# Layer 1 of a graph attention network: rows of each tile divided among TensorE, VectorE and ScalarE by a small search, diagonals in pairs of rows, an earlier store of x and a moved softmax

## The chip, the cores and the metric

The kernel runs on one core of a Trainium2 chip. The metric is device time in microseconds (us) of one execution, median of several runs. Before the change it is 5647.59 us (11 runs, 5640.64 to 5659.87).

## The reference, cut to what matters

A graph of 10,000 nodes and 170,000 directed edges (80,000 random pairs in both directions and one self-loop per node); x is 10,000 x 768, everything in float32. Two attention layers (the first with 4 heads of 256 channels, the second with one head of 768) and a layer norm at the end:

```python
def gat_conv(x, edge_index, W, a_src, a_dst, bias, heads, out_ch, concat):
    xl = (x @ W).reshape(n, heads, out_ch)
    e = leaky_relu(alpha_src[src] + alpha_dst[dst], 0.2)   # alpha: xl times a, per head
    e = exp(e - segment_max(e, dst)[dst])
    alpha = e / (segment_sum(e, dst)[dst] + 1e-16)
    return segment_sum(xl[src] * alpha[:, :, None], dst) + bias
h  = relu(layer_norm(gat_conv(x, W1, ...))) + (x @ Wr1 + br1)        # layer 1, 1024 wide
h2 = layer_norm(gat_conv(h, W2, ...)) + (h @ Wr2 + br2)              # layer 2, 768 wide
out = layernorm(x + h2)
```

## The kernel before

**Stages.** First, until about 884 us of the profile, x @ W1 and the logits go into a table in HBM, `table1` (one row of 1024 + 9 numbers a node), while the nodes are sorted by degree. Then layer 1 (`ordered_layer1`) runs to about 3460 us, and layer 2 (`ordered_layer2`) to the end at 5649 us. The change is in layer 1 alone.

**Tiles of layer 1.** The sorted nodes make 79 tiles of 128. Each partition holds one node. A tile has `SLOTS[t]` = n slots: slot 0 is the node itself, the others are its neighbours, so that a tile takes n gathers of 128 table rows (529 KB each). Worked out from `slot_counts`, the sizes in the order of work climb from 8 to 26, then comes one tile of 41, and then they fall from 27 to 9. How many tiles have each size: 8, 9, 10: one each; 11 and 12: 3 each; 13: 5; 14: 6; 15: 8; 16: 7; 17: 8; 18: 7; 19: 7; 20: 6; 21: 4; 22: 4; 23 and 24: 2 each; 25, 26, 27, 41: one each; 1377 slots in all. The tile of 41 doesn't fit the ring and goes in three parts through `attend_parts`.

**The ring.** Gathered rows lie in a ring of `RING1` = 29 slots in SBUF. `Ring.fetch` (L449, its DMAs at L424) issues the gather for slot q on GpSimd (POOL) once the row that lay there 29 slots earlier is used. Gathers are issued strictly in order.

**The softmax of a tile.** `weights_of(t)` is a generator. Its first step is `logits` (L471 to L490: add, leaky relu, maximum, subtraction on VectorE, exp at L485 on ScalarE); it needs all n rows of the tile. Its second step is `normalised` (L492 to L499, VectorE) and the diagonals and matmuls of the first two rows that TensorE takes; its third step those of the remaining rows. It is called inside the loop of the tile before, so that program order fixes where it stands in each engine's queue: `logits` before row n-3 of the running tile is weighed, `normalised` before row n-2, the third step at the start of the next tile, behind the instruction group `deviation`.

**Three ways to add a row.** Each row of a tile has to be multiplied by its four weights and added to the accumulator `acc` in PSUM:

- on TensorE (L719 to L732): ScalarE makes four diagonal matrices of 128 x 128 from the weights (L723), TensorE multiplies the row by them and adds in PSUM (L729). The first `on_pe(t)` rows go this way: at most 4. They start the accumulation, so VectorE adds its first row only when they are done.
- on VectorE alone (L519): four instructions that multiply and add.
- shared: ScalarE multiplies the row in place (`multiply`, L508, four instructions), VectorE adds it (L515, one instruction).

Of the rows that TensorE leaves, every fourth, beginning with the first, is done by VectorE alone (`shared(t, k)`, `SHARE` = 4). ScalarE multiplies `LEAD` = 3 rows ahead of VectorE (`multiplied`).

**Around the rows.** Tile t - 1 is finished at the start of tile t: statistics on VectorE (L572, L574) and their square root on ScalarE (L576, L577), then `h` (L586, L588, L800), its transposes on TensorE (L699), copies of these on ScalarE (L700), the product with `w2` (L817, `to_layer2`) and the copy of its result (L759) into `row`, which is stored. The transposes of x for tile t (L699 too, copies L700) and the product with `wr1` (L171) stand in between. Two PSUM buffers named `half` serve the transposes and the product with `w2`. x rows of the next tile are gathered into the single buffer `xt` by the event `next_x`, two rows into the loop, and stored to `x_d` for layer 2 by `from_x` (L707) at the start of the next tile.

**Order.** The scope is a `manual_schedule`: every engine runs its instructions in the order of the program, and waits by semaphores where data of other engines is needed. DMAs on the SP queue are issued in program order: `row` (L761), x (L707), `h1_d` (L812).

## Time and profile before

| | us |
|---|---|
| median of 11 runs | 5647.59 |
| profiled execution, its own time | 5650.69 |
| its span | 5648.8 |
| layer 1, about 884 to 3460 | 2576 |
| of that, busy: TensorE / VectorE / ScalarE / POOL | 2267 / 2221 / 1858 / 1479 |

How long one tile of layer 1 takes, as the distance from one L800 to the next in the timeline (means over the tiles of that size):

| rows n | 13 | 14 | 15 | 16 | 17 | 18 | 19 | 20 | 21 | 22 | 23 | 24 | 25 | 26 | 27 |
|---|---|---|---|---|---|---|---|---|---|---|---|---|---|---|---|
| us | 25.9 | 26.3 | 28.2 | 28.3 | 29.6 | 30.6 | 31.9 | 34.1 | 35.8 | 40.0 | 42.4 | 43.5 | 45.4 | 41.9 | 52.1 |

How to read the profile: times are microseconds; PE is TensorE, PEld its weight loads, DVE VectorE, ACT ScalarE, POOL GpSimd, SP the engine that issues most DMAs. A line of the timeline has the start, the length, the engine, the line of the kernel, the operation, the tiles it writes and reads, shapes, how many instructions were merged, and in brackets how long the engine was idle before and what ended that.

### The profile page before, as it was taken

To read this page: it belongs to the slowest core of one execution; us is meant where nothing else is said; L and a number is where in the kernel's file an instruction comes from. 1 tells how busy PE (TensorE), PEld (TensorE's weight loads), DVE (VectorE), ACT (ScalarE), POOL (GpSimd) and SP (SyncE) were. 2 spreads that over 40 slices of the span, in tenths; PEclk is the share of its full clock that TensorE was granted. 3 is DMA by queue.
4 is the path that set the end of the run, shared out by engine and by line. 5 is a ranking of instruction groups with operands and counts; after the bars stand their busy time and mean duration, and the time that the engine had idled before them with its cause. 6 is when DMAs were issued, how large, how long until landed. Compare 5 with 4: busy or idle time off the path is not lost. (4 is left out here: it accounts for less than half of the span.)

```text
span 5648.8 us, 59565 instructions
## 1 busy us (share of the span) xinstructions
PE 4905.3 (87%) x15188; PEld 2901.7 (51%) x15191; DVE 4289.5 (76%) x7729; ACT 2810.0 (50%) x8184; POOL 3225.7 (57%) x3159
## 2 busy tenths in 40 slices
PE   9999996999999865789999999998887757788898
PEld 3444443555555543455555555655555535455565
DVE  5883344999998886888999995886766656777787
ACT  3443344777777766777877763332222222222232
POOL 3447454555666655566666543666656656666563
PEclk9999998999999987899999999998888878888899
DMA  4333627899999986899999986998888878888885
GB/s 155 121 101 86 93 92 264 320 337 353 359 371 357 352 317 221 320 348 353 364 352 356 334 289 254 324 333 303 308 290 287 290 244 301 301 295 299 302 320 201
DMA packets 474307, 1591.37 MB, mean 282 GB/s; under 512 B 118328, under 2 KB 122488, under 8 KB 473959
## 3 DMA queue, kind: packets, MB, share of 16 engines
q0 software_dynamic: 322384, 1286.62, 63.9%
q1 hardware_dynamic: 149520, 297.43, 15.7%
q10 hardware_dynamic: 2054, 3.42, 0.2%
q8 instruction: 128, 2.10, 0.1%
q14 instruction: 221, 1.80, 0.1%
HBM read 1431.80 MB, written 177.29 MB: 285 GB/s over the span
## 5 line engine op out<-in xcount | busy, mean ns | idle before, releaser
L424 POOL DMA_INDIRECT ring<-table,slots x2675 | 2646.4, 989 | 1757.7 <-issue 520.7
L519 DVE SCALAR_TENSOR_TENSOR acc<-ring,e,acc 128x512 f32<-128x512 f32 (+1 forms) x2530 | 1578.3, 624 | 150.8 <-PE acc L729 49.6
L508 ACT ACTIVATE ring<-ring,e 128x256 f32<-128x256 f32 x3284 | 1337.6, 508 | 0.0
L515 DVE TENSOR_TENSOR acc<-acc,ring 128x1024 f32<-128x1024 f32 x801 | 985.6, 1230 | 71.0 <-issue 0.9
L942 PE MATMUL big<-wr,w 128*128 128x512 f32 (+1 forms) x2464 | 895.1, 508 | 160.9 <-issue 159.1
L928 PE MATMUL big<-ring,diagonals 128*128 128x256 f32 x2754 | 735.9, 426 | 187.3 <-issue 150.0
L171 PE MATMUL big<-w,xT 128*128 128x512 f32 x1896 | 826.2, 598 | 21.9 <-DMA w<-in_W_dram 9.2
L171 PE MATMUL big<-wr,xT 128*128 128x512 f32 x1896 | 834.4, 597 | 0.2 <-issue 0.2
L817 PE MATMUL half<-w,hT 128*128 128x512 f32 (+1 forms) x2528 | 830.5, 486 | 0.0
L942 PEld LDWEIGHTS big<-wr,w 128*128 128x128 f32 x2464 | 487.2, 199 | 536.6 <-issue 505.0
L928 PEld LDWEIGHTS big<-ring,diagonals 128*128 128x128 f32 x2754 | 583.2, 215 | 345.4 <-issue 217.8
L927 ACT ACTIVATE diagonals<-ident,e 128x128 f32<-128x128 f32 x1377 | 424.4, 388 | 639.5 <-remote 252.8
L729 PE MATMUL acc<-ring,diagonals 128*128 128x256 f32 x1912 | 485.6, 412 | 223.4 <-ACT diagonals L723 165.8
L817 PEld LDWEIGHTS half<-w,hT 128*128 128x128 f32 x2528 | 477.8, 189 | 372.7 <-issue 329.1
L171 PEld LDWEIGHTS big<-w,xT 128*128 128x128 f32 x1896 | 362.3, 192 | 481.4 <-issue 464.3
L171 PEld LDWEIGHTS big<-wr,xT 128*128 128x128 f32 x1896 | 357.5, 192 | 420.8 <-issue 420.8
L729 PEld LDWEIGHTS acc<-ring,diagonals 128*128 128x128 f32 x1912 | 391.9, 208 | 309.7 <-ACT diagonals L723 182.8
L576 ACT ACTIVATE sd<-mv,eps 128x1 f32<-128x1 f32 x237 | 69.3, 292 | 715.2 <-DVE mv L574 439.0
L723 ACT ACTIVATE diagonals<-ident,e 128x128 f32<-128x128 f32 x956 | 292.8, 387 | 206.7 <-DVE e L499 143.4
L660 DVE TENSOR_TENSOR scr<-big,ad_b 128x1024 f32<-128x1024 f32 x79 | 96.7, 1224 | 375.6 <-ACT row L657 311.2
L665 POOL TENSOR_TENSOR row<-row,none 128x1024 f32<-128x1024 f32 x79 | 187.2, 2369 | 261.4 <-ACT row L657 255.7
L485 ACT ACTIVATE e<-e 128x68 f32<-128x68 f32 (+29 forms) x160 | 38.2, 239 | 574.1 <-DVE e L484 283.6
(172 smaller groups left out, 3633.1 us busy)
## 6 DMA issues: line engine op xcount, KB each, us to landing
ring<-table,slots POOLq DMA_INDIRECT x2675
table<-row SPq DMA_DIRECT2D x79, 516.0 KB
h_d<-hT SPq DMA_DIRECT2D x79, 512.0 KB
w<-h_d SPq DMA_DIRECT2D x77, 512.0 KB
table<-row SPq DMA_DIRECT2D x79, 385.0 KB
ring<-table SPq DMA_DIRECT2D x79, 385.0 KB
xT<-in_x_cols_dram SPq DMA_DIRECT2D x79, 384.0 KB
x_d<-xt SPq DMA_DIRECT2D x79, 384.0 KB
```

The source lines that it names most:

```text
L171: nc.tensor.matmul(p[:, c:e], aT[:, j, :], w[:, j, c:e], start=(j == 0), stop=(j == k - 1))
L424: nc.gpsimd.indirect_dma_start(out=to, out_offset=None, in_=table, in_offset=bass.IndirectOffsetOnAxis(ap=index, axis=0), **more)
L508: nc.scalar.activation(row[:, s], row[:, s], AF.Copy, scale=e[:, h:h + 1])
L515: nc.vector.tensor_add(acc[:, :c], acc[:, :c], row[:, :c])
L519: nc.vector.scalar_tensor_tensor(acc[:, s], row[:, s], e[:, h:h + 1], (acc if first is None else first)[:, s], op0=OP.mult, op1=OP.add)
L665: nc.gpsimd.tensor_add(row[:, :C1], row[:, :C1], b1_b)
L723: nc.scalar.activation(diagonals[:, k * H1 + i, :], ident, AF.Copy, scale=e[:, k, i:i + 1])
L729: nc.tensor.matmul(acc[:, c:d], diagonals[:, k * H1 + i, :], ring.slot(q + k)[:, c:d], start=(k == 0 and c % BANK == 0), stop=(k == m - 1 ...
L817: nc.tensor.matmul(q, hT[:, j, :], w2[:, j, c:c + q.shape[1]], start=(j == 0), stop=(j == K1 - 1))
L927: nc.scalar.activation(diagonals[:, k % G, :], ident, AF.Copy, scale=e[:, k, :])
L928: nc.tensor.matmul(to, diagonals[:, k % G, :], ring.slot(FIRST[t] + k)[:, ON_PE2:C2], start=False, stop=(k == n - 1), skip_group_check=True)
L942: nc.tensor.matmul(r[:, c:d], hT[:, j, :], wr2[:, j, c:d], start=False, stop=(j == K1 - 1 and (d < C2 or not whole(t))), skip_group_check= ...
```

## The change

- **Shares.** `balanced(n)` searches over all pairs (rows on TensorE, rows on VectorE alone) for the one whose longest engine, by seven constants (microseconds a tile and a row), is shortest. `on_pe` and `shared` take their numbers from it. Rows on VectorE alone are spread over the tile, the first one standing first as before.
- **Diagonals.** `summed` is now a generator that takes two rows at a time, each pair in one of two buffers of eight matrices; before, one buffer held sixteen. Each pair is a step of `weights_of`.
- **Store of x.** `fetch_x` itself issues the store to `x_d`, directly behind the gather that fills `xt`.
- **Softmax.** `logits` of the next tile stands before row `begin` of the running tile, `normalised` with the first pair before row `begin + 2`, further pairs one row later each. `begin` is n - 5, later where the ring makes the next tile's last row late, and at most n - 2. Where `begin` is n - 2, `normalised` falls into the next tile and stands behind its statistics (L572, L574). In tiles where the softmax was done in time, the remaining diagonals and the first shared row of the new tile are put ahead of the square root of the statistics on ScalarE.

Worked out by `balanced`, rows on TensorE / VectorE alone / shared, before and after:

| n | before | after | | n | before | after |
|---|---|---|---|---|---|---|
| 13 | 1 / 3 / 9 | 1 / 1 / 11 | | 20 | 4 / 4 / 12 | 4 / 3 / 13 |
| 14 | 2 / 3 / 9 | 1 / 1 / 12 | | 21 | 4 / 5 / 12 | 4 / 3 / 14 |
| 15 | 2 / 4 / 9 | 1 / 1 / 13 | | 22 | 4 / 5 / 13 | 5 / 3 / 14 |
| 16 | 3 / 4 / 9 | 2 / 1 / 13 | | 23 | 4 / 5 / 14 | 5 / 3 / 15 |
| 17 | 3 / 4 / 10 | 2 / 2 / 13 | | 24 | 4 / 5 / 15 | 6 / 4 / 14 |
| 18 | 4 / 4 / 10 | 3 / 2 / 13 | | 25 | 4 / 6 / 15 | 6 / 4 / 15 |
| 19 | 4 / 4 / 11 | 3 / 2 / 14 | | 26, 27 | 4 / 6 / 16, 17 | 7 / 5 / 14, 15 |

Tiles of 8 to 12 rows go from 1 / 2 or 3 / rest to 1 / 1 / rest. Over the whole layer (without the tile of 41): on TensorE 227 to 202 rows, VectorE alone 308 to 149, shared 801 to 985.

```diff
+EARLY = 5
+PE_FIXED, PE_ROW = 24.0, 1.86
+DVE_FIXED, DVE_ROW, DVE_SUM = 7.9, 2.15, 1.31
+ACT_FIXED, ACT_ROW, ACT_DIAGONAL = 4.0, 1.65, 1.21
...
             def fetch_x(t):
                 xt = pool.tile([P, D0], F32, name="xt")
                 gather(xt, x[:, :], nodes(t))
+                nc.sync.dma_start(x_d[t], xt)
                 return xt
...
             def from_x(t):
                 xT = pool.tile([P, K0, P], F32, name="xT")
-                moves = halves(xT, xt)
-                nc.sync.dma_start(x_d[t], xt)
-                return xT, moves
+                return xT, halves(xT, xt)
...
+            def balanced(n):
+                def longest(pe, alone):
+                    both = n - pe - alone
+                    return max(PE_FIXED + PE_ROW * pe, DVE_FIXED + DVE_SUM * both + DVE_ROW * alone,
+                               ACT_FIXED + ACT_DIAGONAL * pe + ACT_ROW * both)
+                return min(((pe, alone) for pe in range(1, n) for alone in range(1, n - pe + 1)),
+                           key=lambda s: (longest(*s), s))
+            split = {n: balanced(n) for n in set(SLOTS)}
             def on_pe(t):
-                return min(max(SLOTS[t] // 2 - 5, 1), ON_PE1, SLOTS[t])
+                return split[SLOTS[t]][0]
...
+            def summed(acc, e, q, m):
+                for lo in range(0, m, 2):
+                    hi = min(lo + 2, m)
+                    diagonals = pool.tile([P, 2 * H1, P], F32, name="diagonals", bufs=2)
...
+                    yield acc
...
-                diagonals = pool.tile([P, ON_PE1 * H1, P], F32, name="diagonals")
-                for lo, hi in ((0, min(m, 2)), (min(m, 2), m)):
-                    summed(acc, diagonals, e, FIRST[t], lo, hi, m)
-                    yield acc
+                yield from summed(acc, e, FIRST[t], m)
             def shared(t, k):
-                return (k - on_pe(t)) % SHARE > 0
+                m, alone = split[SLOTS[t]]
+                return (k - m) * alone % (SLOTS[t] - m) >= alone
...
-                if whole and not ready:
-                    ahead = weights_of(t)
-                    ready += itertools.islice(ahead, 2)
...
-                if whole:
+                if len(ready) == 2:
                     e, acc = ready
+                    for _ in ahead:
+                        pass
+                    multiplied(first + 2)
                 if last:
                     r_before, means = last
                     stats = deviation(small, pieces(means[:, :C1], BANK))
+                if whole and len(ready) < 2:
+                    if not ready:
+                        ahead = weights_of(t)
+                    ready += itertools.islice(ahead, 2 - len(ready))
+                    e, acc = ready
                 for _ in ahead:
                     pass
...
+                begin = n
                 if whole and t + 1 < NT and SLOTS[t + 1] + LEAD <= ring.size:
+                    begin = min(max(n - EARLY, n + SLOTS[t + 1] - ring.size + EARLY), n - 2)
                     ahead = weights_of(t + 1)
                 for k in range(n if whole else 0):
                     multiplied(k + 1 + LEAD)
-                    if n - LEAD <= k < n - LEAD + 2:
-                        ready += itertools.islice(ahead, 1)
+                    if k == begin or k > begin + 1:
+                        step = list(itertools.islice(ahead, 1))
+                        ready += step[:2 - len(ready)]
                     if k >= first:
                         weigh(acc, ring.slot(FIRST[t] + k), e[:, k], DH1, shared=shared(t, k))
...
-                ready += itertools.islice(ahead, max(2 - len(ready), 0))
```

More of the change, by code (lines that the diff above doesn't have):

```diff
@@ L712, in ordered_layer1 @@
             g1_b, be1_b = (spread(pool, v, n) for v, n in ((g1, "g1"), (be1, "be1")))
-            def on_pe(t):
-                return min(max(SLOTS[t] // 2 - 5, 1), ON_PE1, SLOTS[t])
-            def summed(acc, diagonals, e, q, lo, hi, m):
-                for k in range(lo, hi):
-                    for i in range(H1):
-                        nc.scalar.activation(diagonals[:, k * H1 + i, :], ident, AF.Copy,
-                                             scale=e[:, k, i:i + 1])
-                for k in range(lo, hi):
-                    for i in range(H1):
-                        c, d = i * DH1, (i + 1) * DH1
-                        nc.tensor.matmul(acc[:, c:d], diagonals[:, k * H1 + i, :], ring.slot(q + k)[:, c:d],
-                                         start=(k == 0 and c % BANK == 0),
-                                         stop=(k == m - 1 and (d % BANK == 0 or d == C1)),
-                                         skip_group_check=True)
+            def balanced(n):
[5 more added lines that the diff above has]
+                           key=lambda s: (longest(*s), s))
@@ new lines, in ordered_layer1 @@
+            split = {n: balanced(n) for n in set(SLOTS)}
+            def on_pe(t):
+                return split[SLOTS[t]][0]
[3 more added lines that the diff above has]
+                    diagonals = pool.tile([P, 2 * H1, P], F32, name="diagonals", bufs=2)
+                    for k in range(lo, hi):
+                        for i in range(H1):
+                            nc.scalar.activation(diagonals[:, (k - lo) * H1 + i, :], ident, AF.Copy,
+                                                 scale=e[:, k, i:i + 1])
+                    for k in range(lo, hi):
+                        for i in range(H1):
+                            c, d = i * DH1, (i + 1) * DH1
+                            nc.tensor.matmul(acc[:, c:d], diagonals[:, (k - lo) * H1 + i, :],
+                                             ring.slot(q + k)[:, c:d],
+                                             start=(k == 0 and c % BANK == 0),
+                                             stop=(k == m - 1 and (d % BANK == 0 or d == C1)),
+                                             skip_group_check=True)
+                    yield acc
@@ L842, in some @@
                         m = min(ON_PE1, e.shape[1])
-                        diagonals = pool.tile([P, ON_PE1 * H1, P], F32, name="diagonals")
-                        summed(sums, diagonals, e, q, 0, m, m)
+                        for _ in summed(sums, e, q, m):
+                            pass
                         return sums, m
```

## The prediction

> **What bounds the kernel now.** I read the table of stretches first, then the waits, then the timeline of a tile of 15 rows and of one of 23.
>
> ```profile
> core 0: us, PE busy (x) PEld busy (x) DVE busy (x) ACT busy (x) POOL busy (x), PEclk, DMA share, GB/s
> 1500.00:1800.00 300.00, 283.17 (x962) 172.34 (x961) 271.72 (x443) 235.73 (x640) 191.75 (x188) 0.99 0.98 364
> 2200.00:2500.00 300.00, 223.42 (x714) 137.93 (x714) 244.48 (x381) 214.64 (x571) 171.10 (x173) 0.85 0.89 323
> ```
>
> In the first stretch (tiles of 16 to 20 rows) TensorE, VectorE and the DMA engines are all above 90% and ScalarE at 79%: nothing there has much room. In the second (27 down to 22 rows) every engine is idle for a fifth or more, and TensorE's granted clock is 0.85: here a chain of waits sets the time.
>
> ```profile
> 3116.68 0.25 ACT L485 ACTIVATE e<-e 128x60 f32<-128x60 f32 x1 [3.23 <-DVE e L188]
> 3119.21 2.44 ACT L723 ACTIVATE diagonals<-ident,e 128x128 f32<-128x128 f32 x8 [2.28 <-DVE total L498]
> 3124.03 0.29 ACT L576 ACTIVATE sd<-mv,eps 128x1 f32<-128x1 f32 x1 [2.37 <-DVE mv L574]
> 3124.46 0.84 ACT L759 COPY row<-half 128x512 f32<-128x512 f32 x2
> 3127.67 0.86 ACT L700 COPY xT<-half 128x512 f32<-128x512 f32 x2 [0.76 <-PE half L699]
> ...
> 3100.34 1.75 PE L699 MATMUL half<-ident,h 128*128 128x128 f32 x8 [2.29 <-DVE h L800]
> 3101.88 11.51 PE L171 MATMUL big<-wr,xT 128*128 128x512 f32 x24
> 3128.31 1.09 PE L699 MATMUL half<-ident,h 128*128 128x128 f32 x8 [0.46 <-ACT xT L700]
> ```
>
> A tile of 15 rows. VectorE shows no idle time at all in its timeline from 3098.97 (one L800) to 3126.88 (the next): it is the bound. A row alone takes 2.16 us there (3100.11 to 3102.27), a shared row 1.31 (three in 3.94). ScalarE is idle in three places, each time for a VectorE result: 3.2 us before the exp, 2.3 before the diagonals, 2.4 before the square root. The first is true slack; the other two come from the order of the queue. The TensorE lines show one more thing: after 2.29 us of idleness the same eight transposes take 1.75 instead of 1.09, and L171 about 1 us longer; the clock was granted at half for 3.4 us.
>
> ```profile
> 2384.12 0.21 DVE L477 TENSOR_TENSOR e<-ring 128x48 f32<-128x48 f32 x1 [2.24 <-issue]
> 2388.71 0.25 DVE L499 TENSOR_TENSOR e<-e,total 128x88 f32<-128x88 f32 x1
> 2389.51 9.38 PE L729 MATMUL acc<-ring,diagonals 128*128 128x256 f32 x32 [9.33 <-ACT diagonals L723]
> 2391.41 1.29 DVE L572 BATCH_NORM_STATS2 st<-acc 128x6 f32<-128x512 f32 x2
> 2393.05 1.28 DVE L586 SCALAR_TENSOR_TENSOR h<-acc,mv,g 128x1024 f32<-128x1024 f32 x1
> 2395.84 1.22 DVE L800 SCALAR_TENSOR_TENSOR h<-h,big 128x1024 f32<-128x1024 f32 x1
> 2398.93 1.54 DVE L519 SCALAR_TENSOR_TENSOR acc<-ring,e,acc 128x256 f32<-128x256 f32 x3 [1.88 <-PE acc L729]
> ```
>
> A tile of 23 rows passing to one of 22. The softmax ends at 2388.96 (L499); TensorE, idle for 9.3 us and so at half clock, takes 9.4 us for its four rows; VectorE covers this with its last rows, statistics and h, and still waits 1.88 us before its first row. It also waits for the last gathered row (2.24 us before L477): that gather was issued at 2375.94.
>
> **The change part by part.** The sum is made against the profiled execution, 5650.7 us, which is 3.1 above the median.
>
> *Up to 13 rows (14 tiles).* TensorE keeps one row, VectorE changes two rows from alone to shared: 2 x (2.16 - 1.31) = 1.7 us less for 13 rows. TensorE is next: 24.6 us a tile (966.46 to 991.04 in its timeline, without pauses but one of 0.46), and tiles of 13 take 25.9. The early tiles go at TensorE's pace already. Bounds: 0 to -10 us. I take -3, as ScalarE (below) takes part of it.
>
> *14 to 16 rows (21 tiles).* VectorE: for 15 rows 4 alone + 9 shared become 1 + 13, that is -3 x 2.16 + 4 x 1.31 = -1.2 us; the same for 16, and -0.4 for 14. TensorE loses a row, 1.73 us (3.46 for two). ScalarE gains four shared rows of 1.61 us (24 instructions in 9.69) and loses four diagonals (1.22): +5.2. Of the 8 us that it idles, which remain? From the end of `normalised` (time 0): three shared rows on VectorE (3.93) and statistics (1.58) put the square root at 5.5; before it ScalarE now does diagonals (1.2) and one row (1.6) and waits 2.6 for it. Then root 0.43, copies of `row` 0.73, a wait of some 0.5 for TensorE's transposes of x (the row that stood in between is now ahead of the root), xT 0.74: 7.9. Then 11 rows, 17.8; hT 0.95; exp 0.26; and `normalised` 1.2 behind it: 28.1 for a tile that now takes 28.2. So the new rows on ScalarE eat what VectorE saves. With 12 shared rows (14) the same chain gives 26.5 against 26.3; with 16 rows TensorE's two rows delay the copies of xT and it is 28.1 to 29 against 28.3. Bounds: -20 (VectorE's saving alone) to +21 (1 us a tile). I take +7, nearest to the chain.
>
> *17 to 21 rows (32 tiles).* VectorE saves 0.4 (17, 18, 19) to 1.7 (21); ScalarE's +3.6 fits into its 6 to 9 us of idleness. Against it stand the DMA engines: their share is 0.98, no byte is saved, so that a tile of 30 to 34 us has 0.6 to give (-19). With faster rows the wait at L477 comes back: from the freeing of the last slot to landing took 8.2 us in the tile of 23 (2375.94 to 2384.12), the five rows kept in between give 6.6 to 7.4, so 0.8 us. The store of x ends POOL's wait for `xt` (73.7 us in 26 waits in the table of waits). It lies beside compute where rows land early and shortens the landing where they land late. Bounds: -35 (each tile down to VectorE's sum) to +15. I take -10.
>
> *22 to 27 rows (11 tiles).* Here `begin` is n - 2 in the tile before, `normalised` stands behind the statistics, and TensorE gets 5 to 7 rows. VectorE's rows: -3.0 us for 22 and 23 (six tiles), -3.5 for 24 (two), -4.3, -4.8, -4.7 for 25, 26, 27: -39 in all. But what covered the sums is gone: between `normalised` and the first row VectorE now has only L586, L588, L800, 3.9 us. TensorE needs 0.55 to start and, after its pause, 2.2 us for the half clock plus 1.73 a row: 10.8 for five, 12.6 for six, 14.3 for seven. So VectorE waits 7.4, 9.2 or 10.9 us; over six, three and two tiles 94 us, where the idle time before L519 adds up to 21 us in these tiles now: +73. The wait for landing (29 us in them now) stays about as it is: logits come a row later, but rows also free slots closer together. After the tile of 41 the statistics move into a wait: -1.6. Sum +32, taken as +30. Bounds: -18 (TensorE at full clock, no wait for landing) to +42.
>
> *Two buffers of diagonals.* From five rows on, the third pair waits for TensorE's first pair; ScalarE is ready for it at 4.9 us, TensorE done with the first at about 5.6. Some 1 us on ScalarE, which has 10 us idle there: nothing.
>
> *Sum:* -3 + 7 - 10 + 30 = +24, so 5674.7 for a profiled execution and 5671 as the median.
>
> **A rule weighed.** The trace's clock rows: of the tiles of 15 rows, most with TensorE pauses of 2.3 us show half clock and those with 1.8 do not; tiles of 20 rows pause 2.1 to 3.3 us and show it nearly each time, tiles of 16 to 19 pause 1 us or less and never do. With one or two rows less on TensorE and an equal tile time these pauses grow past 2 us. [...]
>
> **The rivals.**
>
> *Faster: the shares do what their row costs say.* For it: VectorE without a gap in tiles of 13 to 17 rows, and its row durations. If ScalarE's queue keeps pace and landing isn't late, the first three groups give about -50; with the large tiles at +8, 5650.7 - 42 = 5609, median 5606. Against it: ScalarE's two waits that the order forces, and the DMA share of 0.98.
>
> *The two ends cancel.* ScalarE half in the way (-25) and large tiles +25: 5648. For it: four resources within 3% of each other in the first stretch, so that none can give much.
>
> *Much slower: ScalarE becomes the bound of all middle tiles.* If a shared row waits for ScalarE in the 41 tiles of 14 to 20 rows at 0.8 us each (+33), with the large tiles at +30: 5714, median 5711. It decides from the point where ScalarE's idle time before the exp is gone. Against it: from 17 rows on that time should last.
>
> **How the numbers follow.** Forecast (around 5671): 0.40. Much slower: 0.15. Cancelling: 0.20. Faster: 0.25. A measurement of this kernel tells about 0.2% (11 us) from no change, so faster 0.25, same 0.2, slower 0.55. The range runs from 5612 (near the faster case, whose outer half is left out) to 5710 (the much slower one). The likeliest case's own range is 5655 to 5690, its large tiles between +15 and +42.
>
> **What would show it.** Right: VectorE idle before its first row (L519 before) in tiles of 22 to 27 rows at 7 us and more; ScalarE without idle time before the exp in tiles of 14 to 16; half clock still there from 20 rows on; tiles of 15 rows at 28, tiles of 24 at 46 to 49; no wait of POOL for the store of x. Wrong: tiles of 15 and 16 rows at 27 (ScalarE wasn't in the way), or tiles of 22 to 25 rows shorter than now (the moved softmax costs less than its cover).

## The result, and the profile after

The changed kernel takes 5703.96 us (median of 8 runs, 5689.99 to 5721.23), against 5650.71 us of the kernel before (30 runs by then): a ratio of 1.0097, 95% interval 1.0086 to 1.0108. It is slower, by some 53 us. Its profiled execution has a span of 5722.1 us, 73.3 more than that of before. Layer 1 explains 59 of these: its last `h` (L800 before, L822 after) starts at 3490.5 instead of 3431.2 us. The other 14 lie in layer 2, whose code is the same: from the last `h` to the end of the span the kernels of this study on chips of the same speed took between 2204 and 2232 us without any order, so I compare layer 1 alone, tile by tile, from the line of one `h` to the next.

Lines moved a little: the gather is L428 now, `logits` begins at L481, exp is L489, `normalised` is L506 (its first instruction) to L503, the multiply on ScalarE L512, the shared add L519, a row on VectorE alone L523, the root L580, the copies of transposes L705, the diagonals L740, their matmuls L746.

The change of the tile times, added up over the tiles of each size, beside what the forecast gave:

| rows | tiles | forecast, us | measured, us |
|---|---|---|---|
| up to 13 | 14 | -3 | +1.4 |
| 14 to 16 | 21 | +7 | +9.7 |
| 17 to 21 | 32 | -10 | +9.3 |
| 22 to 27 | 11 | +30 | +38.9 |
| 41 | 1 | (in the line above) | -0.9 |
| sum | | +24 | +58.4 |

The stretches of the kernel after (columns: busy time and number of instructions of each engine, granted TensorE clock, DMA share, GB/s):

```profile
core 0: us, PE busy (x) PEld busy (x) DVE busy (x) ACT busy (x) POOL busy (x), PEclk, DMA share, GB/s
1500.00:1800.00 300.00, 276.87 (x901) 162.76 (x900) 266.72 (x386) 272.03 (x719) 195.34 (x190) 0.97 0.98 362
2200.00:2500.00 300.00, 201.85 (x686) 133.06 (x685) 206.86 (x325) 207.26 (x562) 166.74 (x166) 0.84 0.82 295
```

In the first stretch ScalarE went from 235.73 to 272.03 us: it is now as busy as VectorE and TensorE, while the bytes moved per second are the same. In the second every engine is busy for about two thirds, VectorE 38 us less than before, and the DMA rate fell from 323 to 295 GB/s: the chain of waits became longer.

A tile of 15 rows after, from the timeline (start, length, engine, line, operation, tiles, idle time before and what ended it):

```profile
3161.65 12.88 ACT L512 ACTIVATE ring<-ring,e 128x256 f32<-128x256 f32 x32
3174.42 0.25 ACT L489 ACTIVATE e<-e 128x60 f32<-128x60 f32 x1
3174.56 1.71 ACT L512 ACTIVATE ring<-ring,e 128x256 f32<-128x256 f32 x4
3176.16 1.28 ACT L740 ACTIVATE diagonals<-ident,e 128x128 f32<-128x128 f32 x4
3181.26 0.29 ACT L580 ACTIVATE sd<-mv,eps 128x1 f32<-128x1 f32 x1 [2.22 <-issue]
...
3174.71 0.23 DVE L506 TENSOR_SCALAR e<-e,loops 128x4 f32<-128x4 f32 x1 [0.94 <-issue]
...
3157.63 1.07 PE L704 MATMUL half<-ident,h 128*128 128x128 f32 x8 [2.29 <-ACT ring L512]
```

ScalarE, which idled 3.2 us before the exp, comes to it straight from its rows (two instructions of a tile's timeline overlap by some 0.1 us). VectorE, without any idle time before, now waits 0.94 us for that exp before it can normalise. The tile takes 27.86 us; before it was 28.24 in the mean. So this size still gained a little: the +9.7 us of the group lie in the six tiles of 14 rows (+6.6) and the seven of 16 (+4.1), while the eight of 15 are 1.0 shorter, because what VectorE saves there is more than it waits.

The passage from the last tile of 24 rows to the last of 23. Before the change (the lines in the prediction are of the next passage, from 23 to 22 rows):

```profile
2357.37 2.06 DVE L519 SCALAR_TENSOR_TENSOR acc<-ring,e,acc 128x256 f32<-128x256 f32 x4 [2.46 <-PE acc L729]
...
2347.36 9.97 PE L729 MATMUL acc<-ring,diagonals 128*128 128x256 f32 x32 [10.17 <-ACT diagonals L723]
```

And after:

```profile
2395.75 0.29 ACT L580 ACTIVATE sd<-mv,eps 128x1 f32<-128x1 f32 x1 [4.28 <-DVE mv L578]
2396.89 4.78 ACT L740 ACTIVATE diagonals<-ident,e 128x128 f32<-128x128 f32 x16 [0.62 <-DVE e L503]
2403.67 1.28 ACT L740 ACTIVATE diagonals<-ident,e 128x128 f32<-128x128 f32 x4 [1.99 <-PE acc L746]
...
2396.60 0.25 DVE L503 TENSOR_TENSOR e<-e,total 128x92 f32<-128x92 f32 x1
2399.55 1.22 DVE L822 SCALAR_TENSOR_TENSOR h<-h,big 128x1024 f32<-128x1024 f32 x1
2408.85 2.06 DVE L523 SCALAR_TENSOR_TENSOR acc<-ring,e,acc 128x256 f32<-128x256 f32 x4 [8.08 <-PE acc L746]
...
2397.34 11.47 PE L746 MATMUL acc<-ring,diagonals 128*128 128x256 f32 x40 [10.96 <-ACT diagonals L740]
```

The softmax ends at 2396.85 (L503), and only `h` stands between it and the first row of VectorE, which waits 8.08 us for five rows on TensorE, where it waited 2.46 for four. TensorE, idle for 11 us, is at half clock again (its granted clock is 0.50 from 2389 to 2402 us), as it was before after 10 us (0.50 from 2339.5 to 2353). The third pair of diagonals does wait 1.99 us for a buffer, but TensorE's 40 matmuls run on without a gap, so that nobody pays for it.

A tile of 21 rows shows what the forecast did not have at all:

```profile
2560.48 0.24 DVE L503 TENSOR_TENSOR e<-e,total 128x84 f32<-128x84 f32 x1
2563.24 0.21 DVE L578 BATCH_NORM_AGGREGATE mv<-st 128x2 f32<-128x12 f32 x1
2567.59 1.28 DVE L592 SCALAR_TENSOR_TENSOR h<-h,sd,be 128x1024 f32<-128x1024 f32 x1 [2.76 <-ACT sd L581]
...
2560.76 4.78 ACT L740 ACTIVATE diagonals<-ident,e 128x128 f32<-128x128 f32 x16 [3.86 <-DVE total L502]
2565.45 1.69 ACT L512 ACTIVATE ring<-ring,e 128x256 f32<-128x256 f32 x4
2567.04 0.28 ACT L580 ACTIVATE sd<-mv,eps 128x1 f32<-128x1 f32 x1
```

The statistics are there at 2563.45, but ScalarE has sixteen diagonals and a shared row in front of the root, which starts 3.6 us later; VectorE waits 2.76 us for it before the second step of `h`.

Added up from the timeline, VectorE's idle time in layer 1 by what it waited for (us, before to after; a sum is good to about 1 us, by how small gaps are counted):

| waiting for | 14 to 16 | 17 to 21 | 22 to 27 |
|---|---|---|---|
| TensorE's rows, before the first row | 1.1 to 0.7 | 19.9 to 3.4 | 21.0 to 97.0 |
| landing, before `logits` | 0 | 3.8 to 18.0 | 29.5 to 20.6 |
| the root, before the second step of `h` | 0.5 to 0 | 0 to 17.4 | 0 to 2.8 |
| exp, before `normalised` | 0 to 19.0 | 2.5 to 4.3 | 0 |
| a row from ScalarE (L515 before, L519 after) | 1.0 to 12.4 | 0.5 to 18.2 | 1.0 to 9.3 |

### The profile page after: what moved, and what is told of

Read it like the earlier page. It is cut to its first block, busy times and chain, and to the rows that moved or that the text cites. A ratio compares the mean times of both kernels' runs of the same rounds, so it can differ in the third digit from the quotient of the medians.

```text
span 5722.1 us, 59341 instructions
## 1 busy us (share of the span) xinstructions
PE 4901.7 (86%) x14988; PEld 2885.5 (50%) x14991; DVE 4205.2 (73%) x7277; ACT 3072.6 (54%) x8820; POOL 3225.4 (56%) x3159
## 5 line engine op out<-in xcount | busy, mean ns | idle before, releaser
L428 POOL DMA_INDIRECT ring<-table,slots x2675 | 2643.1, 988 | 1899.1 <-issue 561.9
L512 ACT ACTIVATE ring<-ring,e 128x256 f32<-128x256 f32 x4020 | 1644.3, 505 | 1.5 <-issue 1.5
L523 DVE SCALAR_TENSOR_TENSOR acc<-ring,e,acc 128x512 f32<-128x512 f32 (+1 forms) x1894 | 1267.5, 669 | 189.6 <-PE acc L746 108.2
L519 DVE TENSOR_TENSOR acc<-acc,ring 128x1024 f32<-128x1024 f32 x985 | 1212.0, 1230 | 119.1 <-ACT ring L512 21.4
L175 PE MATMUL big<-wr,xT 128*128 128x512 f32 x1896 | 863.4, 613 | 0.2 <-ACT xT L705 0.2
L951 ACT ACTIVATE diagonals<-ident,e 128x128 f32<-128x128 f32 x1377 | 425.5, 388 | 652.5 <-remote 275.1
L746 PE MATMUL acc<-ring,diagonals 128*128 128x256 f32 x1712 | 433.2, 413 | 228.0 <-ACT diagonals L740 201.0
L175 PEld LDWEIGHTS big<-wr,xT 128*128 128x128 f32 x1896 | 369.8, 199 | 439.3 <-issue 438.6
L746 PEld LDWEIGHTS acc<-ring,diagonals 128*128 128x128 f32 x1712 | 355.1, 209 | 298.4 <-ACT diagonals L740 210.3
L580 ACT ACTIVATE sd<-mv,eps 128x1 f32<-128x1 f32 x237 | 69.2, 292 | 676.3 <-DVE mv L578 352.6
L667 ACT ACTIVATE scr<-scr 128x256 f32<-128x256 f32 x632 | 253.5, 402 | 120.3 <-DVE scr L664 120.3
L740 ACT ACTIVATE diagonals<-ident,e 128x128 f32<-128x128 f32 x856 | 260.1, 389 | 91.2 <-DVE e L503 58.2
```

The lines of the kernel that those rows point to most:

```text
L175: nc.tensor.matmul(p[:, c:e], aT[:, j, :], w[:, j, c:e], start=(j == 0), stop=(j == k - 1))
L428: nc.gpsimd.indirect_dma_start(out=to, out_offset=None, in_=table, in_offset=bass.IndirectOffsetOnAxis(ap=index, axis=0), **more)
L512: nc.scalar.activation(row[:, s], row[:, s], AF.Copy, scale=e[:, h:h + 1])
L519: nc.vector.tensor_add(acc[:, :c], acc[:, :c], row[:, :c])
L523: nc.vector.scalar_tensor_tensor(acc[:, s], row[:, s], e[:, h:h + 1], (acc if first is None else first)[:, s], op0=OP.mult, op1=OP.add)
L667: nc.scalar.activation(m[:, s], m[:, s], AF.Copy, accum_out=row[:, C1 + i * H1 + h:C1 + i * H1 + h + 1])
```

## The experiments

Theory A is the explanation by parts: in large tiles the moved softmax leaves the sums of TensorE bare, in tiles of 14 to 16 rows ScalarE is too full. The first four kernels ran on one chip, the next four on another, the last four on a third; each is compared with runs of the kernel before on its own chip. Tile times are compared with the profile of before that is shown above. On the first chip the kernel before takes 5343.19 us; the tile of 10 rows, the first that can be timed, is 6 to 11 us longer there in all four kernels, and is left out of their first column. The ratio of each kernel, and the change of the tile times in us:

| kernel | ratio to before, 95% interval | up to 13 | 14 to 16 | 17 to 21 | 22 to 27 |
|---|---|---|---|---|---|
| changed kernel | 1.0097 (1.0086 to 1.0108) | +1.4 | +9.7 | +9.3 | +38.9 |
| e1 shares alone | 1.0044 (1.0030 to 1.0059) | +3.5 | +21.6 | +0.8 | -7.7 |
| e2 softmax alone | 1.0080 (1.0063 to 1.0097) | +0.4 | -4.9 | +22.4 | +26.7 |
| e3 store alone | 0.9994 (0.9984 to 1.0003) | +1.7 | -1.1 | -7.3 | -3.3 |
| e4 changed, 22 rows and more as before | 1.0036 (1.0022 to 1.0050) | +0.9 | +7.1 | +3.5 | +1.2 |
| e5 changed, root first from 19 rows on | 1.0078 (1.0061 to 1.0095) | +0.9 | +6.2 | +9.5 | +39.0 |
| e6 changed, softmax as before from 22 on | 1.0044 (1.0029 to 1.0059) | +1.0 | +6.3 | +12.3 | +8.7 |
| e7 changed, shares of 14 to 16 as before | 1.0074 (1.0054 to 1.0095) | +2.5 | -1.6 | +2.4 | +37.3 |
| e8 parts chosen by size | 0.9985 (0.9975 to 0.9994) | | | | |
| e9 changed, order as before from 17 on | 1.0040 (1.0028 to 1.0051) | +2.2 | +7.8 | +8.8 | +7.5 |
| e10 changed, at most 4 rows on TensorE | 1.0070 (1.0049 to 1.0090) | -0.1 | +9.7 | +14.9 | +25.6 |
| e11 one row less alone | 0.9946 (0.9928 to 0.9963) | -2.3 | -10.7 | -12.9 | +6.2 |
| e12 the same, large shares as before | 0.9959 (0.9944 to 0.9973) | -2.3 | -11.6 | -15.1 | +0.2 |

The tile times are those of one execution each; groups that an edit leaves alone differ between kernels, which is the measure for smaller differences. The group of 14 to 16 rows has the same shares and order in the changed kernel, e4, e5, e6, e9 and e10 and lies between +6.2 and +9.7; that of 17 to 21 rows has the same shares and order in the changed kernel, e4, e6, e7 and e10 and lies between +2.4 and +14.9, so that there a difference of some 6 us from the changed kernel says nothing. e8's profiled execution took 5693 us, far from its median of 5645, and is not used.

### Each part alone: e1, e2, e3

Shares and pairs of diagonals in the kernel before, with its order and its store:

```diff
+            split = {n: balanced(n) for n in set(SLOTS)}
...
-                return min(max(SLOTS[t] // 2 - 5, 1), ON_PE1, SLOTS[t])
+                return split[SLOTS[t]][0]
...
-                return (k - on_pe(t)) % SHARE > 0
+                m, alone = split[SLOTS[t]]
+                return (k - m) * alone % (SLOTS[t] - m) >= alone
```

> The shares and the pairs of diagonals alone; softmax, order at the start of a tile and store of x as before. Theory A (the place of the softmax and what it leaves uncovered costs the time; the shares alone need the earlier softmax, because ScalarE then idles for the statistics instead of multiplying a row): the tiles of 22 to 27 rows come out near before (between -15 and +15 us in all, VectorE waiting about 3 us, not 8, before its first row), the tiles of 14 to 19 rows 1 to 2 us longer each, +40 to +70 us in all. Rival B (184 more rows on ScalarE cost the time in every tile, wherever the softmax stands): as much as the whole change, +45 to +65 us, with the tiles of 22 to 27 rows at +30 or more.

The place of the softmax and the order at the start of a tile, with the old shares:

```diff
-                if whole and not ready:
-                    ahead = weights_of(t)
-                    ready += itertools.islice(ahead, 2)
...
+                if len(ready) == 2:
+                    e, acc = ready
+                    for _ in ahead:
+                        pass
+                    multiplied(first + 2)
...
+                    begin = min(max(n - EARLY, n + SLOTS[t + 1] - ring.size + EARLY), n - 2)
...
-                    if n - LEAD <= k < n - LEAD + 2:
-                        ready += itertools.islice(ahead, 1)
+                    if k == begin or k > begin + 1:
```

> The moved softmax and the new order at the start of a tile alone; rows shared as before, at most four on TensorE, diagonals in one buffer, store of x as before. Theory A: tiles of 22 to 27 rows wait about 6 us before the first row (four rows on TensorE at half clock at first, 9.1 + 0.55 - 3.9) against 1.9 now, less the wait for landing that shrinks: +20 to +35 us in these, +0 to +10 in tiles of 20 and 21 from the square root standing behind the diagonals, nothing in tiles of 13 to 17 where VectorE has no gap: +20 to +45 us in all. Rival B: the move costs nothing by itself, -15 to +10 us.

The store alone:

```diff
                 gather(xt, x[:, :], nodes(t))
+                nc.sync.dma_start(x_d[t], xt)
...
-                nc.sync.dma_start(x_d[t], xt)
```

> Only the store of x issued at its landing. Theory A: POOL's waits for the buffer of x (73.7 us in 26) go and nothing else follows, -6 to +3 us, since VectorE, not landing, ends most tiles. Rival C (the store now falls among the gathers of the next tile's last rows and makes them land later): +10 to +20 us, seen as longer waits before the first softmax instruction in tiles of 18 to 25 rows.

The store makes no difference that can be measured (0.9994, interval across 1), as forecast: POOL's 73.7 us of waiting for it lay beside other work.

The shares alone cost 0.44%, 21 us, less than either theory expected, and their loss lies in 14 to 16 rows, one microsecond a tile. The timeline of a tile of 15 rows of that kernel (lines there are one lower):

```profile
3113.84 14.48 ACT L511 ACTIVATE ring<-ring,e 128x256 f32<-128x256 f32 x36
3128.21 0.26 ACT L488 ACTIVATE e<-e 128x60 f32<-128x60 f32 x1
3133.72 0.29 ACT L579 ACTIVATE sd<-mv,eps 128x1 f32<-128x1 f32 x1 [2.71 <-DVE mv L577]
...
3120.38 1.23 DVE L518 TENSOR_TENSOR acc<-acc,ring 128x1024 f32<-128x1024 f32 x1 [0.36 <-ACT ring L511]
3128.50 0.23 DVE L505 TENSOR_SCALAR e<-e,loops 128x4 f32<-128x4 f32 x1 [1.35 <-ACT e L488]
```

From row to row VectorE waits 0.36 us for ScalarE (1.60 from one shared row to the next, against the 1.31 that it needs itself), and 1.35 for the exp; ScalarE still waits 2.71 us for the statistics. It is full in one place and forced idle in another. In large tiles the new shares alone, 5 to 7 rows on TensorE, lost nothing (-7.7).

The softmax alone does what theory A said of large tiles (+26.7, expected +20 to +35), and something that it didn't say: +22.4 in 17 to 21 rows, 12 of them in the seven tiles of 19. A tile of 19 of that kernel:

```profile
2705.02 1.23 DVE L516 TENSOR_TENSOR acc<-acc,ring 128x1024 f32<-128x1024 f32 x1
2709.88 0.24 DVE L478 TENSOR_TENSOR e<-ring 128x76 f32<-128x76 f32 x1 [3.62 <-DMA ring<-table,slots]
```

`logits` needs every row of the next tile; two rows earlier, the last one has not landed, and VectorE stands for 3.62 us. In the 32 tiles of 17 to 21 rows the wait grew from 3.8 to 33.8 us. In 14 to 16 rows, where the ring holds the next tile early, the same order saves 4.9, no more than groups differ anyway.

### The large tiles: e4, e6, e10

In the changed kernel, shares and order of tiles of 22 rows and more put back:

```diff
-            split = {n: balanced(n) for n in set(SLOTS)}
+            split = {n: as_before(n) if n >= 22 else balanced(n) for n in set(SLOTS)}
...
-                    for _ in ahead:
-                        pass
-                    multiplied(first + 2)
+                    if n < 22:
+                        for _ in ahead:
+                            pass
+                        multiplied(first + 2)
...
+                    if SLOTS[t + 1] >= 22:
+                        begin = n - LEAD
```

> The whole change, but tiles of 22 rows and more share their rows, place their softmax and order their start as before. Theory A: the 39 us that these tiles gained go away, the rest of the +55 stays: +10 to +25 us against before. Rival B: the loss is spread over all tiles, +35 us or more remain.

The same with the new shares kept, so that only the place of the softmax is put back:

```diff
+                    if n < 22:
+                        for _ in ahead:
+                            pass
+                        multiplied(first + 2)
...
+                    if SLOTS[t + 1] >= 22:
+                        begin = n - LEAD
```

> The whole change, but for tiles of 22 rows and more the softmax stands where it stood before (logits before row n-3, normalised before row n-2, root ahead of the rest); they keep the new shares with 5 to 7 rows on TensorE. Theory A: the loss of 39 us in these tiles comes from the place of the softmax, so it turns into a gain of 0 to 10 us as with the shares alone: +5 to +15 us against before in all. Rival B': five to seven rows on TensorE at half clock cost it, wherever the softmax stands: +35 us or more.

The new place kept, and the search held to four rows on TensorE:

```diff
-                return min(((pe, alone) for pe in range(1, n) for alone in range(1, n - pe + 1)),
+                return min(((pe, alone) for pe in range(1, min(n, ON_PE1 + 1)) for alone in range(1, n - pe + 1)),
```

> The changed kernel with one bound in its search: at most four rows on TensorE, so that tiles of 22 to 27 rows have 4 instead of 5 to 7 there (18 rows less in 11 tiles) and nothing else changes. Theory A (with the softmax moved, each further row on TensorE stands bare in front of VectorE's first row, at 1.73 us): the wait before the first row falls by 18 x 1.73 = 31 us in these tiles, VectorE gets 19 us of rows back, so the group goes from +38.9 to about +27, and the whole is 8 to 16 us faster than the changed kernel. Rival B (the wait is that of the place alone, or other waits take over): the group stays at +35 and more.

All put back: +1.2, and the whole is 20 us above before, as theory A expected. The place alone put back: +8.7, so 30 of the 39 us go with the place. The rows held to four at the new place: +25.6, and VectorE's wait before the first row in these tiles falls from 97.0 to 64.0 us, 33 where 18 rows of 1.73 give 31; the whole is 8.5 us faster than the changed kernel, as theory A expected, though the intervals of the two ratios overlap. The two parts of the 39 us, 30 for the place and 13 for the rows, overlap and don't add up to it. The same wait, at the passage to the last tile of 23 rows, in e10:

```profile
2397.52 2.06 DVE L523 SCALAR_TENSOR_TENSOR acc<-ring,e,acc 128x256 f32<-128x256 f32 x4 [5.43 <-PE acc L746]
...
2388.66 8.82 PE L746 MATMUL acc<-ring,diagonals 128*128 128x256 f32 x32 [13.52 <-ACT diagonals L740]
```

8.08 us became 5.43, 2.65 less, and so did the sums themselves (11.47 to 8.82): in this tile the fifth row is on the path at its full length. e6 as a whole, +27 us, lies above the +5 to +15 that theory A had expected of it, because its other groups stay slower; rival B', +35 or more, does not hold either.

### 14 to 16 rows: e7

```diff
-            split = {n: balanced(n) for n in set(SLOTS)}
+            split = {n: as_before(n) if 14 <= n <= 16 else balanced(n) for n in set(SLOTS)}
...
+                if 14 <= SLOTS[t] <= 16:
+                    return (k - m) % SHARE > 0
```

> The whole change, but tiles of 14, 15 and 16 rows share their rows as before. Theory A: four more rows on ScalarE make it the bound in these 21 tiles; without them they come out at 26 to 28.1 us, 5 us below before in sum instead of 10 above: 10 to 17 us faster than the whole change. Rival: VectorE is the bound there and loses its 0.4 to 1.2 us a tile again: 10 to 20 us slower than the whole change.

The group goes from +9.7 to -1.6, and the whole gains 11.5 us on the changed kernel (5692.42), as theory A expected, though here too the intervals of the two ratios overlap. VectorE's waits for the exp, 19.0 us, and for rows of ScalarE, 12.4, go to 0 and 0.5; 4.9 us of waiting for TensorE's rows come in their place. So the twelve or thirteen shared rows were the cause there.

### 17 to 21 rows: e5, e9

First the wait for the root, taken away: from 19 rows on, the root stands in front of the diagonals again.

```diff
                 if len(ready) == 2:
                     e, acc = ready
-                    for _ in ahead:
-                        pass
-                    multiplied(first + 2)
+                    if n < 19:
+                        for _ in ahead:
+                            pass
+                        multiplied(first + 2)
```

> The whole change, but in tiles of 19 rows and more ScalarE takes the square root of the statistics ahead of the remaining diagonals and of the first shared row, as before. Theory A: VectorE's wait for the root before its second step of h (17 us in tiles of 17 to 21 rows, 3 in larger ones) goes: 10 to 20 us faster than the whole change. Rival: the wait only hides another (TensorE's sums, which end about as late), 0 to -4 us against the whole change, with the wait found again before the first row.

Theory A missed and its rival held: the whole is 4 us faster than the changed kernel, within the uncertainty, and the group stays at +9.5. A tile of 21 rows in e5:

```profile
2560.91 1.28 DVE L592 SCALAR_TENSOR_TENSOR h<-h,sd,be 128x1024 f32<-128x1024 f32 x1
2562.30 1.22 DVE L823 SCALAR_TENSOR_TENSOR h<-h,big 128x1024 f32<-128x1024 f32 x1
2566.86 2.07 DVE L523 SCALAR_TENSOR_TENSOR acc<-ring,e,acc 128x256 f32<-128x256 f32 x4 [3.33 <-PE acc L746]
```

The wait for the root is gone and 3.33 us have appeared two instructions further, before the first row. In the 32 tiles the root's 17.4 us became 0.5, and the first row's 3.4 became 22.7. The root was never the bound: VectorE would have waited for TensorE's rows next.

Then the order put back for 17 rows and more, with all new shares:

```diff
+                    if n < 17:
+                        for _ in ahead:
+                            pass
+                        multiplied(first + 2)
...
+                    if SLOTS[t + 1] >= 17:
+                        begin = n - LEAD
```

> The changed kernel with all its shares; only where the softmax of a tile of 17 and more rows stands, and the place of the root and the first shared row at the start of such a tile, are as before. Theory A (the shares are harmless from 17 rows on, the earlier logits and the later root cost what the 17 to 21 rows lost): the group of 17 to 21 rows goes from +9.3 to between -5 and +4, the group of 22 to 27 from +38.9 to about +9, 14 to 16 stays near +8: layer 1 some 15 to 25 us longer than before the change. Rival B (ScalarE's extra shared rows cost it, wherever the softmax stands): 17 to 21 rows stay at +7 to +12, layer 1 some 27 to 35 us longer.

The group stays at +8.8, which is what rival B expected of it; layer 1, +26 us, lies just between the two theories, and the sizes within the group don't agree. Tiles of 18 to 21 rows go from +10.3 in the changed kernel to +1.0, as theory A said, but tiles of 17 go from -1.0 to +7.9. The landing wait falls from 18.0 to 2.5 us and the root's from 17.4 to 1.0; the wait for ScalarE's rows grows from 18.2 to 37.3. The same tile of 18 rows before the change:

```profile
2764.32 0.26 ACT L485 ACTIVATE e<-e 128x72 f32<-128x72 f32 x1 [1.35 <-DVE new L481]
2767.08 2.45 ACT L723 ACTIVATE diagonals<-ident,e 128x128 f32<-128x128 f32 x8 [2.49 <-issue]
```

And in e9:

```profile
2773.52 1.23 DVE L519 TENSOR_TENSOR acc<-acc,ring 128x1024 f32<-128x1024 f32 x1 [0.77 <-ACT ring L512]
2775.11 1.23 DVE L519 TENSOR_TENSOR acc<-acc,ring 128x1024 f32<-128x1024 f32 x1 [0.36 <-issue]
...
2771.76 14.49 ACT L512 ACTIVATE ring<-ring,e 128x256 f32<-128x256 f32 x36
2786.13 0.28 ACT L489 ACTIVATE e<-e 128x72 f32<-128x72 f32 x1
2787.81 2.44 ACT L740 ACTIVATE diagonals<-ident,e 128x128 f32<-128x128 f32 x8 [1.40 <-DVE total L502]
2791.79 0.29 ACT L580 ACTIVATE sd<-mv,eps 128x1 f32<-128x1 f32 x1 [1.54 <-DVE mv L578]
```

No idle time is left before the exp, and 1.40 and 1.54 us of forced idle time remain; VectorE waits 0.77 and then 0.36 us a row for ScalarE. So with the order of before, too, the new shares win nothing from 17 rows on (e1: +0.8). The 8 us of the tiles of 17 rows are a wait of VectorE for the exp, 7.4 us in these tiles in e9 and none in e1. Why it appears in e9 only, when e1 has the same shares and nearly the same order there but the late store, and ran on another chip, was not settled.

### Versions that follow from this: e8, e11, e12

e8 keeps the new shares only for 17, 18 and 22 rows and more, the new order only below 19 rows, and the early store:

```diff
+            kept = set(range(1, 17)) | {19, 20, 21}
+            split = {n: as_before(n) if n in kept else balanced(n) for n in set(SLOTS)}
...
+                    if n < 19:
...
+                    if SLOTS[t + 1] >= 19:
+                        begin = n - LEAD
```

> Each part where theory A says that it pays: new shares for 17, 18 and 22 to 27 rows, shares as before elsewhere; softmax moved and the new order at the start up to 18 rows, as before from 19 on; x stored at its landing. By the groups of the runs before: up to 16 rows -5, 17 and 18 rows -8, 19 to 21 rows -5, 22 to 27 rows -8: 15 to 30 us faster than before. If the parts don't add up (rival B): within 10 us of before.

Only 5 us faster than before the change: rival B's range holds, and the parts don't add up.

e11 leaves TensorE's rows as they were up to 21 rows and turns one row of VectorE's into a shared one; the order is the new one below 17 rows:

```diff
+            def one_less(n):
+                pe = min(max(n // 2 - 5, 1), ON_PE1, n)
+                return pe, max(-(-(n - pe) // SHARE) - 1, 1)
+            split = {n: one_less(n) if n < 22 else balanced(n) for n in set(SLOTS)}
...
+                    if n < 17:
...
+                    if SLOTS[t + 1] >= 17:
+                        begin = n - LEAD
```

> A version by what the runs showed: rows on TensorE as before up to 21 rows, and one row of VectorE's alone made a shared one; the shares of the search from 22 rows on; softmax where it stood before from 17 rows on and where the change puts it below; x stored at landing. Theory A (a single further shared row fits into ScalarE's queue): VectorE saves 0.85 us in each of the tiles of 13 to 16 rows (26 tiles, -22 at most, half of it reached), tiles of 17 to 21 give -5 to -20 (the DMA share bounds them), the large ones -8 to +5: 15 to 40 us faster than before. Rival B (TensorE and the DMA engines are as near to the bound as VectorE): no more than 5 us faster.

It takes 5624.97 us, 25.6 less than before the change and 79 less than the changed kernel. Its first stretch, and a tile of 15 rows (L744 is the diagonals there):

```profile
core 0: us, PE busy (x) PEld busy (x) DVE busy (x) ACT busy (x) POOL busy (x), PEclk, DMA share, GB/s
1500.00:1800.00 300.00, 286.39 (x990) 176.53 (x989) 266.66 (x417) 254.89 (x690) 193.49 (x189) 0.99 0.98 368
```

```profile
3102.12 0.25 ACT L489 ACTIVATE e<-e 128x60 f32<-128x60 f32 x1 [0.18 <-issue]
3106.73 2.44 ACT L744 ACTIVATE diagonals<-ident,e 128x128 f32<-128x128 f32 x8 [2.76 <-DVE e L503]
3112.05 0.29 ACT L580 ACTIVATE sd<-mv,eps 128x1 f32<-128x1 f32 x1 [1.28 <-issue]
...
3105.51 0.22 DVE L506 TENSOR_SCALAR e<-e,loops 128x4 f32<-128x4 f32 x1
```

In this tile one more row fits: ScalarE arrives at the exp with 0.18 us to spare, and `normalised` follows on VectorE without a wait. It doesn't fit everywhere without cost: VectorE waits 18 us for rows of ScalarE in the tiles of 17 to 21 rows (0.5 before). And e11 also has the early store, and the new order below 17 rows; no kernel has the one row alone, so that its part of the 25.6 us isn't measured by itself. The tiles of 15 rows take 27.28 us, those of 17 to 19 are 0.6 to 0.8 us shorter than before the change, and the DMA engines move 368 GB/s, 4 more than before, at the same share of 0.98.

e12 is e11 with the old shares in tiles of 22 rows and more:

```diff
-                return pe, max(-(-(n - pe) // SHARE) - 1, 1)
-            split = {n: one_less(n) if n < 22 else balanced(n) for n in set(SLOTS)}
+                return pe, max(-(-(n - pe) // SHARE) - (n < 22), 1)
+            split = {n: one_less(n) for n in set(SLOTS)}
...
+                if SLOTS[t] >= 22:
+                    return (k - m) % SHARE > 0
```

> The version with one row of VectorE's alone made a shared one, but with the shares of before in tiles of 22 rows and more, so that 4 rows of them are on TensorE and not 5 to 7. The order is as before there in both. Theory A (5 to 7 rows on TensorE cost something even where the softmax stands as before, as the tiles of 24 to 27 rows showed in the version before this one): the group of 22 to 27 rows goes from +6.2 to between -3 and +2, and the whole is 4 to 9 us faster than that version, 28 to 35 us faster than before the change. Rival B (that +6 is noise of its execution, and the search's shares save VectorE time there, as where the shares alone were put in): the group goes to +10 and more, and the whole is slower than that version.

The large tiles go from +6.2 to +0.2, and before the first row VectorE waits 19.4 us in them instead of 57.6. The whole (5629.69 against 5654.11 of before beside it, 24 us faster where theory A expected 28 to 35) can't be told from e11: the intervals overlap. That the new shares cost 6 to 9 us in large tiles at the old place (e6, e9, e11) and gained 7.7 in e1 stays open; e1 has the late store and ran on another chip, and its landing wait there was 20 us instead of 30.

## Why the prediction was right or wrong

The direction and the range held, and the change is slower for the two reasons given, the bare sums of TensorE in large tiles and ScalarE's queue in tiles of 14 to 16 rows. The size was missed: the forecast (5671) was 33 us short, most of that by one step, and 5704 lies above the likeliest case's own range (5655 to 5690) and nearer to the much slower rival (5711). That the wide range held it owes to that rival, which set its upper end, not to the sum.

*22 to 27 rows: right.* The uncovered wait was forecast as 94 us against 21 and is 97.0 against 21.0; it lies at 7.0 to 8.2 us in tiles of 22 and 23, 9.1 and 10.2 in those of 24, 9.8 to 10.9 from 25 on. VectorE's rows: the four waits together grew by 78.2 us (76.0 - 8.9 + 2.8 + 8.3) and the tiles by 38.9, so the rest, which is not measured by itself, gave back 39.3; the forecast had 39. Three smaller terms were not in the sum: shared rows that wait for ScalarE at the start of a tile, where the copies of xT and hT stand between its rows (8.3), the root (2.8), and a landing wait that became 8.9 less where no change was forecast. Together they are +2.2. The rest of the 9 us by which the group exceeds the forecast is the wait (+76 instead of +73), the -1.6 of the tile of 41, which the forecast counted in this term, and its rounding of +32 to +30.

*14 to 16 rows: right.* The chain on ScalarE was forecast at 28.1 us for 15 rows and measured 28.12; at 28.1 to 29 for 16 (28.83); at 26.5 for 14 (27.45, which is the term that was short). There is no idle time before the exp, and e7 shows that these shares were the cause.

*17 to 21 rows: wrong.* Forecast -10, measured +9.3 (+2.4 to +14.9 in the five kernels with these shares and this order): more than half of the whole error. The step that failed is "ScalarE's +3.6 fits into its 6 to 9 us of idleness". Of these 6 to 9 us (6.9 in the mean) only the wait before the exp is free time, 61.9 us over 32 tiles or 1.9 a tile; the waits before the diagonals (2.8) and the root (1.9) are forced by the order, as the prediction itself had said of the tile of 15 rows. A net load of 3.6 us doesn't fit into 1.9: in e1 and e9, with the order of before, the wait before the exp falls to 0.2 us a tile, the two forced ones only from 4.8 to 3.3 and 3.5, VectorE waits 36 and 37 us for ScalarE's rows, and nothing is gained. One more row of 1.6 us fits better (e11, with that order and the early store: this group at -12.9, 18 us of waiting for ScalarE's rows). Beside that, the price of an earlier `logits`, taken as 0.8 us against a saving, was too small: the landing wait in these tiles grew by 14 us in the changed kernel, and by 30 where the move stands alone (e2). The root's place, which the sum did not have, cost nothing of its own (e5).

*Up to 13 rows.* Forecast -3, measured +1.4, just outside the bounds of 0 to -10. The mechanism named (ScalarE takes part) holds: VectorE waits 14.6 us for the exp in these tiles, where it did not before.

*Two buffers, store of x: right.* A wait for the buffer is there (1.99 us at the passage shown) and nobody pays for it; the store alone can't be measured, and POOL's wait for it, 73.7 us, is gone from the table of waits.

*Of the rivals,* the faster one fell, as ScalarE's queue did not keep pace, which was its condition. The one in which the two ends cancel needed -25 us from the tiles up to 21 rows, and these gave +20; its ground, four resources within 3% of each other, doesn't stand in the row it is read from either, which has TensorE at 94%, VectorE at 91%, the DMA engines at 98% and ScalarE at 79%. The one in which ScalarE bounds all middle tiles came partly true: its condition, no idle time before the exp, holds in tiles of 14 to 16 rows and nearly in those of 17 to 21 (61.9 to 8.8 us), but its price was at most the 19.0 us by which these 53 tiles grew, 0.36 each and not 0.8. (It counted 41 tiles of 14 to 20 rows; by the list of sizes there are 49, which at 0.8 would have been +39 and not +33.)

*Pauses and the granted clock.* Pauses of TensorE grew past 2 us in tiles of 13 to 19 rows, as said, and the clock rows show what follows. The same stretch (20 down to 16 rows) before and after, columns as above:

```profile
2646.00:3100.00 454.00, 430.41 (x1468) 258.38 (x1467) 413.57 (x671) 350.59 (x944) 283.67 (x277) 1.00 0.98 358
```

```profile
2646.00:3100.00 454.00, 415.95 (x1353) 244.62 (x1351) 407.95 (x592) 409.89 (x1080) 287.74 (x282) 0.97 0.98 361
```

The granted clock fell from 1.00 to 0.97 of full speed. In tiles of 13 to 19 rows, 30 pauses of 2.0 to 2.5 us are in the trace after, and 23 of them show half clock, granted for 3.4 or 6.8 us at a time; before there were 4 such pauses, and 3 of them did. Shorter pauses, of 0.3 to 1.9 us, number 39 after, and half clock lies beside at most 7 of them, each within 4 us of a longer pause. Before, the tiles of 16 to 19 rows paused up to 1.5 us, a little more than the forecast read, and none showed it. From 880 to 3470 us half clock took 365 us instead of 282. So half clock went with most pauses of little more than 2 us here, and not with all of them. What half clock cost can't be seen in like tiles: three of 15 rows with it at their start took 27.84 to 27.88 us and the two without it 27.85 and 27.86, as TensorE was not the bound in them: it paused 2.29 or 2.30 us at the start of all five. Three more with it took 28.29 to 29.10, and what made these longer was not traced.

## What to carry to other kernels

An engine's idle time is room for new work only where it stands in front of something that can come earlier; a wait that the order of the queue forces stays for the most part when the engine gets more to do (3.3 to 3.5 of 4.8 us a tile in e1 and e9). So divide rows among engines by the chain through a tile, with its waits, and not by sums of busy time: here one more shared row a tile belonged to a version that gained 0.5% (e11), and shares with one to four more cost 0.4% (e1). And work that starts an accumulation needs cover on the engine that waits for it (VectorE's wait for TensorE's rows in large tiles went from 21.0 to 97.0 us here): when it is moved, count what is left between its release and the first use.

## What the runs showed that was not expected

- TensorE fell to half clock after pauses of 2.0 to 2.5 us in 23 of 30 cases, and several of these tiles took no longer than like ones without it (15 rows: 27.84 to 27.88 us against 27.85 and 27.86).
- One of the chips runs layer 2 much faster: between 4000 and 5000 us of its profile (e3, whose code differs from before only in the store) the DMA engines move 334 GB/s at a share of 0.93, against 289 at 0.84 of the kernel before on another, and the kernel before takes 5343 us there instead of 5650. Layer 1 is the same on both, 2489.6 us from its first to its last `h` against 2489.3.
- A wait taken away from VectorE came back two instructions later at nearly the same size (e5: 17.4 us of one, 19.3 of the other).
